# Splitting the products with C by a running difference, and loading batch norm rows over 128 partitions, in a four-layer hybrid kernel

## The chip, the cores and the metric

The kernel runs on one core of a Trainium2 chip. Its time is the time on the device, in microseconds. The kernel before the change took 6,203.77 us (median of three runs, 6,194.5 to 6,205.01). The engines are called PE (TensorE), DVE (VectorE), ACT (ScalarE), POOL (GpSimd) and SP (SyncE, which issues the DMAs here).

## What is computed

Four images of 96 channels and 64 x 64 pixels pass through four layers: a selective scan (layer 0), an inverted bottleneck with a depthwise convolution (layer 1), a spectral mixer with a quantised feed-forward (layer 2), and linear attention with another quantised feed-forward (layer 3). The change concerns layer 0's scan and the constants of layers 1 and 2. The scan, for each image, each of K = 4 directions, each of 192 channels d and 16 states n, over 4,096 positions:

```
dA  = exp(delta[d, t] * A[d, n])
h   = h * dA + (delta[d, t] * u[d, t]) * B[n, t]
y[d, t] = sum over n of h[d, n, t] * C[n, t]
```

The batch norms of layers 1 and 2 are affine maps that the kernel folds into the weights next to them: `s = g * rsqrt(v + eps)`, `t = b - m * s`, and then the weight matrix times `s` with `t` as one more row. As g, b, m and v are wanted along a matrix's columns, each is loaded as a row that is repeated over the partitions.

## The kernel before

**Units and steps.** The scan is cut into 64 steps: four images, four directions, four pieces of 1,024 positions. A step has 24 units, numbered u = 0 to 23. A unit is one tile of 128 partitions (32 channels by 4 states) by 1,024 positions, so there are 1,536 units. The loop `for slot in range(len(units) + 6)` (L1363) takes one unit a slot, in an order written out by hand (`manual_schedule`, L1493): each engine runs its instructions in the order in which this loop issues them.

**What a slot issues.** At slot s, in this order: on ACT `keep` (L1305), which copies the last column of unit s-1's state for the next piece, and the exponential of unit s+1 (`decays`, L1286), into one of two PSUM tiles (`da`); on POOL the input product g x B of unit s+2 (`inputs`, L1279), into one of eight tiles `w`; on POOL the product with C of unit s-2, if that unit is one of POOL's; on DVE the scan of unit s (`states`, L1293) and, if the unit is not POOL's, its product with C right behind (`product`, L1308); on PE the sums over states of a pair of units (`sums`, L1331), three slots after the pair's second unit. If a unit is POOL's, its states h are written over w in SBUF, and the product is made in place there; if it is DVE's, h is written over da in PSUM, and the product reads it there and writes w. Which units are POOL's is fixed before: `POOL_C` (L47) lists ten values of u, all even; the other fourteen are DVE's.

**Side work.** All other work (the input convolution and scan inputs of the next images, called the front stage; the convolution block; the spectral stages; layers 2 and 3) is written as generators that yield the engine and a planned time, as `yield dv(0.9)`. Stages follow each other in a plan (L1223). After each slot's own instructions, `advance` (L1454) takes side work whose engine has planned room left in this slot (`SHARE`, L58), up to a rate. The planned times (in us) steer the order alone. Behind the last scan only side work is left.

**The rows.** The first stage beside the scan is `weights` (`later_weights`, L324), which runs together with the group norm statistics of the three later images. It loads g1, b1, m1 and v1 as rows of 576 values and, in a second batch (L383), those of layer 2 as rows of 192 values, each repeated over C + 1 = 97 partitions, by `load_row` (L161), on SP's queue. The group norm statistics (`group_norm`, L509) load pieces of x (L502) and take `bn_stats` of them on DVE (L516).

Of the kernel before, what the change touches and what calls it, by code (L numbers as in the profile page):

```python
# [27 lines left out]
B, C, H, W = 4, 96, 64, 64  # L28
L = H * W
K, NS, R, DI = 4, 16, 6, 192  # L30
NE = R + 2 * NS
HID, NT1 = 576, 5
# [11 lines left out]
KORDER = [(0, 1, 3, 2)] * (B - 1) + [(1, 3, 0, 2)]  # L44

SCAN = {"d": 4, "g": 4, "B": 4, "C": 4, "w": 8}
POOL_C = (0, 2, 4, 6, 8, 12, 14, 16, 18, 20)  # L47
LAST = {"tab": 24, "more": 6}
TMP, IN = 9, 4

# [46 lines left out]
def hybrid_kernel(ctx: ExitStack, tc: tile.TileContext, a: dict):  # L97
# [10 lines left out]
    pool = lambda name, bufs=1, **kw: ctx.enter_context(tc.tile_pool(name=name, bufs=bufs, **kw))  # L108
# [52 lines left out]
    def load_row(out, name):  # L161
        load(out, a["rows"][:, ROW[name]].partition_broadcast(out.shape[0]))
        return out
# [32 lines left out]
    def big(name):  # L196
        if last_room and turns(thirds) == "last":
            return last_room[0].tile([128, 6144], F32, name=name, tag="big", bufs=1)
        return bp.tile([128, 6144], F32, name=name, tag="big", bufs=2)
# [86 lines left out]
    def scratch(t):  # L286

        at = 0

        def take(parts, *shape):  # L290
            nonlocal at
            n = int(np.prod(shape))
            at += n
            out = t[:parts, at - n : at]
            return out if len(shape) == 1 else out.rearrange("p (a b) -> p a b", b=shape[1])

        return take
# [26 lines left out]
    def later_weights():  # L324
# [3 lines left out]
        take = scratch(big("weights"))  # L328
        wo_a, wo_b = take(128, C), take(64, C)
        load(wo_a, a["wout_t"][0:128])  # L330
        load(wo_b, a["wout_t"][128:DI])
        s1, t1 = take(C + 1, HID), take(C + 1, HID)
        g1, b1, m1, v1 = (load_row(take(C + 1, HID), n) for n in ("g1", "b1", "m1", "v1"))
        g2r, v2r = load_row(take(128, C), "g2"), load_row(take(128, C), "v2")
        yield wait(4)
        yield pe(1.0, 1)
# [40 lines left out]
        take = scratch(big("weights"))  # L377
# [1 line left out]
        load(pre, a["pre"])  # L379
        w1t = take(C, DI)  # L380
        load(w1t, a["wa1_t"])
        sa, ta = take(C + 1, DI), take(C + 1, DI)
        ga, ba, ma, va = (load_row(take(C + 1, DI), n) for n in ("bn1_g", "bn1_b", "bn1_m", "bn1_v"))  # L383
        g, v = load_row(take(128, C), "bn2_g"), load_row(take(128, C), "bn2_v")
        load_row(rdid[0:64], "rd")
        load_row(rdid[64:128], "id")
# [3 lines left out]
        n = 2 * NG  # L390
# [35 lines left out]
        take = scratch(big("weights"))  # L426
# [27 lines left out]
    def flush():  # L454
        while to_store:
            out, t, then = to_store.pop(0)
            store(out, t)
            if then is not None:
                then()
# [772 lines left out]
    def scans(stages):  # L1232
# [13 lines left out]
        units = []  # L1246
        for number, step in enumerate(steps):
            u = 0
            for which, chans in enumerate(PASSES):
                for j in range(NJ):  # L1250
                    for i in chans:
                        units.append({"step": step, "number": number, "u": u, "j": j, "i": i, "pass": which,
                                      "pool": u in POOL_C})
                        u += 1

        def fetch(step, name, i):
            t = step[name][i] = wide(name)
            if name in "BC":
                lo = 4 * i + (NS if name == "C" else 0)
                of = d_bc[step["k"]][step["b"] % 3][step["c"], lo : lo + 4].unsqueeze(0)  # L1260
            else:
                of = (d_delta if name == "d" else d_du)[step["k"]][step["b"] % 3]
                of = of[step["c"], 32 * i : 32 * i + 32].unsqueeze(1)
            load(t, of.to_broadcast([32, 4, CH2]))

        def need(step):

            while not traced[step["b"]].issuperset((step["k"] % 2, 2 * step["c"] + e) for e in (0, 1)):
                force(stages)
            flush()  # L1270
# [6 lines left out]
        def inputs(x):  # L1277
            x["w"] = wide("w")
            nc.gpsimd.tensor_mul(x["w"], x["step"]["g"][x["i"]], x["step"]["B"][x["j"]])  # L1279

        def decays(x, last):
            if last is not None:
                keep(last)
            av = (x["step"]["k"] * NI + x["i"]) * NJ + x["j"]
            x["da"] = decay_banks()
            act(x["da"], x["step"]["d"][x["i"]], AF.Exp, scale=aneg[:, av : av + 1])  # L1286

        def states(x):
            step, u = x["step"], x["u"]
            order = slice(None, None, -1) if step["k"] >= 2 else slice(None)  # L1290
            x["h"] = x["w"] if x["pool"] else x["da"]
            start = 0.0 if step["n"] == 0 else steps[x["number"] - 1]["last"][:, u : u + 1]
            nc.vector.tensor_tensor_scan(  # L1293
                x["h"][:, order], x["da"][:, order], x["w"][:, order], start, ALU.mult, ALU.add
            )
            if not x["pool"]:
                product(x, nc.vector)
# [9 lines left out]
        def product(x, engine):  # L1307
            x["made"] = engine.tensor_mul(x["w"], x["h"], x["step"]["C"][x["j"]])  # L1308
# [31 lines left out]
        def sums_out():  # L1340
            while summed:
                group, y = summed.pop(0)
                step = group[0]["step"]
                yt = sp.tile([128, CH], F32, name="yt", bufs=1)
                nc.scalar.copy(yt, y)  # L1345
                which = group[0]["pass"]
                for e in (0, 1):
                    to = d_y[step["k"]][step["b"] % 2][2 * step["c"] + e]
                    later(to[64 * which : 64 * which + 64], yt[64 * e : 64 * e + 64],
                          (lambda b=step["b"]: through(b)) if which == len(PASSES) - 1 and e == 1 else None)  # L1350
# [12 lines left out]
        for slot in range(len(units) + 6):  # L1363
            clock[0] = slot
            x = units[slot] if slot < len(units) else None
            if x is not None:
                if x["u"] == 0:


                    last = len(units) - NST * PC  # L1370
                    if slot < last:
                        rate = max(RATE, sum(s.work for s in stages if s not in behind) / (last - slot))
                    else:
                        rate = sum(s.work for s in stages) / (len(units) - slot)
                for name, i in OWN.get(x["u"], ()):
                    fetch(x["step"], name, i)
                if x["number"] + 1 < len(steps) and x["u"] in LOADS:
                    if x["u"] == 14:
                        need(steps[x["number"] + 1])
                    for name, i in LOADS[x["u"]]:  # L1380
                        fetch(steps[x["number"] + 1], name, i)
            flush()
            if slot + 1 < len(units):
                decays(units[slot + 1], units[slot - 1] if slot > 0 else None)
            sums_out()
            if slot + 2 < len(units):
                inputs(units[slot + 2])
            if 2 <= slot < len(units) + 2 and units[slot - 2]["pool"]:
                product(units[slot - 2], nc.gpsimd)
            if x is not None:  # L1390
                states(x)
            for group in due.get(slot, ()):
                sums(group)
            for e, (us, most) in SHARE.items():
                room[e] = min(room[e] + us, most)
            tensor[0] = 0.0
            held_banks[0] -= freed[0]
            freed[0] = 0
            owed = min(owed + rate, 8.0)
            while owed > 0.0:  # L1400
                did = advance(stages)
                if did is None:
                    break
                owed -= did
        flush()


    clock, tensor = [-1], [0.0]
    room = {e: most for e, (_, most) in SHARE.items()}

    class Stage:
# [42 lines left out]
    def advance(stages):  # L1454

        while stages and not stages[0].fill():
            stages.pop(0)
        if stages:
            banks_left = BANKS["mm"] - held_banks[0]
            for stream in stages[0].active:  # L1460
                engine, us, banks, _ = stream["next"]
                if banks and banks > banks_left:

                    banks_left = 0
                elif fits(stream):
                    if engine != "wait":
                        room[engine] -= us
                    if engine == "pe":
                        tensor[0] += us
                    return stages[0].step(stream)  # L1470
        return None

# [175 lines left out]
```

## Time and profile before

| | |
|---|---|
| median of three runs | 6,203.77 us |
| the profiled execution | 6,203.38 us, its span 6,201.6 us |
| granted TensorE clock, mean | 0.85 |
| PE busy | 4,590.7 us (74%) |
| DVE busy | 5,318.7 us (86%) |
| ACT busy | 3,841.3 us (62%) |
| POOL busy | 5,069.5 us (82%) |
| products with C on POOL, on DVE | 640, 896 |

The page first gives busy time by engine, then the span in forty slices, the DMA queues, the chain of work that ended last, and the costliest groups of instructions. A group's row has the line, the engine, the operation, the tile written and those read, shapes and count; behind the first bar the busy time in us and the mean of one in ns; behind the second the idle time of the engine just before them, and what ended most of it. A row of the waits names the engine that waited and the line of its instruction, what ended the wait, and then the sum in us, the number of times and the longest. A row of the timeline has the start, the duration, the engine and the instruction, and in brackets the idle time before it; SPq is SP's queue, issuing DMAs.

### The profile page before, as it was taken

What the parts mean: (1) busy time and instruction counts of PE and PEld (TensorE: products, weight loads), DVE (VectorE), ACT (ScalarE), POOL (GpSimd) and SP (SyncE); (2) the same over time, 40 slices, a digit from 0 to 9 for tenths busy, and PEclk for the clock granted to TensorE, in tenths of its full rate; (3) what the DMA queues carried; (4) which work ended last, traced back from release to release, by engine and by line L of the source; (5) the groups of instructions that cost most, each with busy time, mean ns of one, the idle gap of its engine ahead of it and who ended that gap; (6) DMA issues with size and microseconds to landing.
All of it is one profiled execution on the core that took longest, in us unless ns stands there. A gap on an engine that the chain in (4) does not pass through costs nothing. (4 is left out here: it accounts for less than half of the span.)

```text
span 6201.6 us, 78736 instructions
## 1 busy us (share of the span) xinstructions
PE 4590.7 (74%) x27668; PEld 1692.7 (27%) x27668; DVE 5318.7 (86%) x3619; ACT 3841.3 (62%) x6056; POOL 5069.5 (82%) x2183
## 2 busy tenths in 40 slices
PE   6632867755888776686569878767898777678998
PEld 2100212210222542121012236321222542112284
DVE  4979899899999889989999998898999999898045
ACT  4742776764565577767546656777666667675335
POOL 4756878879999899988899998999999899898000
PEclk9765977867999888788779988888999888789999
DMA  5653566567654554456776445557754554674201
GB/s 180 218 168 120 193 201 202 195 213 226 218 167 155 188 166 150 157 189 200 228 228 198 155 149 187 174 174 221 228 162 154 176 183 157 194 223 131 71 13 40
DMA packets 424718, 1078.09 MB, mean 174 GB/s; under 512 B 79258, under 2 KB 81024, under 8 KB 423172
## 3 DMA queue, kind: packets, MB, share of 16 engines
q1 hardware_dynamic: 424324, 1073.06, 54.6%
q8 instruction: 220, 3.60, 0.2%
q14 instruction: 174, 1.43, 0.1%
HBM read 856.64 MB, written 220.66 MB: 174 GB/s over the span
## 5 line engine op out<-in xcount | busy, mean ns | idle before, releaser
L1279 POOL TENSOR_TENSOR scan_w<-scan_g,scan_B 128x1024 f32<-128x1024 f32 x1536 | 3607.5, 2377 | 370.9 <-PE ps_y L1331 281.6
L1286 ACT ACTIVATE ps_da<-scan_d,aneg 128x1024 f32<-128x1024 f32 x1536 | 1714.8, 1117 | 567.6 <-DVE scan_w L1293 294.4
L1293 DVE TENSOR_TENSOR_SCAN ps_da<-ps_da,state,scan_w 128x1024 f32<-128x1024 f32 x672 | 1576.3, 2346 | 199.9 <-ACT ps_da L1286 173.8
L1308 POOL TENSOR_TENSOR scan_w<-scan_w,scan_C 128x1024 f32<-128x1024 f32 x640 | 1519.5, 2374 | 274.3 <-ACT state L1305 163.9
L1331 PE MATMUL ps_y<-scan_w,cst 128*32 128x512 f32 x6144 | 993.2, 725 | 559.1 <-ACT yt L1345 195.7
L1308 DVE TENSOR_TENSOR scan_w<-ps_da,scan_C 128x1024 f32<-128x1024 f32 x896 | 1097.2, 1225 | 67.6 <-DMA scan_C<-bc 4.6
L1293 DVE TENSOR_TENSOR_SCAN scan_w<-ps_da,state,scan_w 128x1024 f32<-128x1024 f32 x480 | 1123.4, 2340 | 28.1 <-ACT ps_da L1286 25.5
L1293 DVE TENSOR_TENSOR_SCAN ps_da<-ps_da,scan_w 128x1024 f32<-128x1024 f32 x224 | 512.0, 2286 | 85.3 <-ACT ps_da L1286 66.8
L1331 PEld LDWEIGHTS ps_y<-scan_w,cst 128*32 128x32 f32 x6144 | 145.8, 117 | 1191.5 <-issue 642.1
L1305 ACT COPY state<-ps_da 128x1 f32<-128x1 f32 x672 | 106.9, 159 | 548.8 <-DVE scan_w L1308 547.3
L1293 DVE TENSOR_TENSOR_SCAN scan_w<-ps_da,scan_w 128x1024 f32<-128x1024 f32 x160 | 364.8, 2280 | 16.9 <-ACT ps_da L1286 9.6
L827 PE MATMUL ps_mm<-h,wd 128*32 128x512 f32 x3144 | 362.9, 593 | 9.0 <-ACT r L167 7.0
L565 PE MATMUL ps_mm<-xp,taps 128*128 128x512 f32 x576 | 292.3, 651 | 59.6 <-ACT xp L545 26.8
L804 PE MATMUL ps_mm<-wd,w 128*32 128x512 f32 x1944 | 241.8, 608 | 22.9 <-ACT h L808 10.7
L616 PE MATMUL ps_mm<-xd,dtw 128*128 128x512 f32 x256 | 167.6, 746 | 87.8 <-ACT z L638 50.3
L886 PE MATMUL ps_mm<-r,cst 128*128 128x512 f32 x220 | 151.0, 775 | 82.1 <-ACT r L883 25.8
L670 PE MATMUL ps_mm<-ya,cst 128*64 128x512 f32 x192 | 183.2, 1044 | 12.8 <-ACT acc L910 11.3
L631 DVE SCALAR_TENSOR_TENSOR ps_mm<-ps_mm,z 128x512 f32<-128x512 f32 x192 | 131.7, 686 | 68.4 <-ACT z L629 68.0
L625 ACT ACTIVATE z<-ps_mm 128x512 f32<-128x512 f32 x192 | 114.1, 594 | 121.9 <-PE ps_mm L620 60.2
L1000 PE MATMUL ps_mm<-wa,xp 128*64 128x96 f32 x1728 | 132.3, 311 | 66.0 <-DVE d L1009 37.5
L565 PEld LDWEIGHTS ps_mm<-xp,taps 128*128 128x128 f32 x576 | 115.3, 207 | 234.2 <-issue 158.4
L827 PEld LDWEIGHTS ps_mm<-h,wd 128*32 128x32 f32 x3144 | 104.3, 109 | 248.7 <-issue 210.9
(360 smaller groups left out, 6553.0 us busy)
## 6 DMA issues: line engine op xcount, KB each, us to landing
scan_g<-du SPq DMA_DIRECT2D x384, 512.0 KB, 4.8
scan_d<-delta SPq DMA_DIRECT2D x384, 512.0 KB, 6.0
scan_B<-bc SPq DMA_DIRECT2D x256, 512.0 KB, 5.0
scan_C<-bc SPq DMA_DIRECT2D x256, 512.0 KB, 5.6
y<-yt SPq DMA_DIRECT2D x384, 128.0 KB, 2.4
du<-g SPq DMA_DIRECT2D x128, 256.0 KB, 2.3
delta<-z SPq DMA_DIRECT2D x128, 256.0 KB, 2.4
tab<-in_etab SPq DMA_DIRECT2D x112, 256.0 KB, 4.6
```

The lines of the kernel that those rows point to most:

```text
L565: mm(p, lhsT=taps[:, t, 0:128], rhs=window(t, c + e), start=t == 0, stop=t == 8)
L616: mm(p, lhsT=dtw[:, o + 2 * third, 0:128], rhs=xd, start=True, stop=True)
L670: mm(split(p[:64]), lhsT=const("two")[:, :64], rhs=t[:, :L].rearrange("p (w h) -> p h w", h=H)[:, c * RPC : (c + 1) * RPC, :], start=True, ...
L804: mm(p[32 * n : 32 * n + 32], lhsT=w1[:, 32 * g : 32 * g + 32], rhs=xin[:, n : n + 15 : 2, 1 : W + 1], start=True, stop=True)
L827: mm(p[32 * n : 32 * n + 32], lhsT=held["wd"][:, groups[i], o, dx, :], rhs=here[i][:, :, dx : dx + W], start=dx == 0, stop=dx == 2)
L886: mm(v, lhsT=const("mean"), rhs=r, start=True, stop=True)
L1000: mm(p[s : s + 64, e * C : (e + 1) * C], lhsT=tok[:, g * 4 + e, :], rhs=wa1[:, hs], start=True, stop=True)
L1279: nc.gpsimd.tensor_mul(x["w"], x["step"]["g"][x["i"]], x["step"]["B"][x["j"]])
L1286: act(x["da"], x["step"]["d"][x["i"]], AF.Exp, scale=aneg[:, av : av + 1])
L1293: nc.vector.tensor_tensor_scan(x["h"][:, order], x["da"][:, order], x["w"][:, order], start, ALU.mult, ALU.add)
L1308: x["made"] = engine.tensor_mul(x["w"], x["h"], x["step"]["C"][x["j"]])
L1331: done = mm(y[32 * q : 32 * q + 32], lhsT=const("stack"), rhs=group[m]["w"][:, e * CH : e * CH + CH], start=first, stop=last)
```

## The change

The list `POOL_C` goes. At each unit `share` decides between the engines by a running difference, `ahead_by`: the planned work of DVE less that of POOL so far. A unit adds a scan on DVE (2.35) and an input product on POOL (2.37); its product with C adds 1.2 on DVE or 2.37 on POOL, and goes where the difference is left nearer to zero. The planned times of DVE's side work are added as `advance` takes them, and the difference is held within 6 us either way. Odd units can now be POOL's, and so can two units in a row. The order of all else is as before.

The rows of both batch norms, and the values s and t made of them, take 128 partitions in place of 97; only 97 of them are read.

```diff
-POOL_C = (0, 2, 4, 6, 8, 12, 14, 16, 18, 20)
+SCAN_US, PRODUCT_US = 2.35, (1.2, 2.37)
+AHEAD = 6.0
...
-        s1, t1 = take(C + 1, HID), take(C + 1, HID)
-        g1, b1, m1, v1 = (load_row(take(C + 1, HID), n) for n in ("g1", "b1", "m1", "v1"))
+        s1, t1 = take(128, HID), take(128, HID)
+        g1, b1, m1, v1 = (load_row(take(128, HID), n) for n in ("g1", "b1", "m1", "v1"))
...
-        sa, ta = take(C + 1, DI), take(C + 1, DI)
-        ga, ba, ma, va = (load_row(take(C + 1, DI), n) for n in ("bn1_g", "bn1_b", "bn1_m", "bn1_v"))
+        sa, ta = take(128, DI), take(128, DI)
+        ga, ba, ma, va = (load_row(take(128, DI), n) for n in ("bn1_g", "bn1_b", "bn1_m", "bn1_v"))
...
-                        units.append({"step": step, "number": number, "u": u, "j": j, "i": i, "pass": which,
-                                      "pool": u in POOL_C})
+                        units.append({"step": step, "number": number, "u": u, "j": j, "i": i, "pass": which})
...
+        def share(x):
+
+            on_vector, on_pool = PRODUCT_US
+            lead = ahead_by[0] + SCAN_US - on_pool
+            x["pool"] = abs(lead - on_pool) < abs(lead + on_vector)
+            lead += -on_pool if x["pool"] else on_vector
+            ahead_by[0] = max(-AHEAD, min(lead, AHEAD))
+
         def states(x):
             step, u = x["step"], x["u"]
+            share(x)
...
                 owed -= did
+                ahead_by[0] += beside[0]
+                beside[0] = 0.0
...
+    beside, ahead_by = [0.0], [0.0]
...
                     if engine == "pe":
                         tensor[0] += us
+                    if engine == "dve":
+                        beside[0] += us
```

## The prediction

> **What bounds the kernel now.** I read first the page's groups and its forty slices, then the stretches of time around what looked odd, then the waits, and last the issue queue. A stretch row holds start:end, its length, then the busy time of PE, PE's weight loads, DVE, ACT and POOL (count in brackets), granted clock, DMA share, GB/s. The groups:
>
> ```profile
> L1279 POOL TENSOR_TENSOR scan_w<-scan_g,scan_B 128x1024 f32<-128x1024 f32 x1536 | 3607.5, 2377 | 370.9 <-PE ps_y L1331 281.6
> L1308 POOL TENSOR_TENSOR scan_w<-scan_w,scan_C 128x1024 f32<-128x1024 f32 x640 | 1519.5, 2374 | 274.3 <-ACT state L1305 163.9
> L1308 DVE TENSOR_TENSOR scan_w<-ps_da,scan_C 128x1024 f32<-128x1024 f32 x896 | 1097.2, 1225 | 67.6 <-DMA scan_C<-bc 4.6
> ```
>
> A product with C is 1.225 us on DVE and 2.374 us on POOL; 640 of 1,536 lie on POOL. The scans themselves are 3,576 us of DVE (the four L1293 groups: 1576.3 + 1123.4 + 512.0 + 364.8). They run from 88.9 us to 5,724 us, so this phase is 5,635 of the 6,201.6 us. What follows is 477 us in which PE is busy for 441.8 us; the change doesn't touch it. Within the phase no engine is the bound throughout. Four steps (a step is 24 units) as stretches:
>
> ```profile
> 653.00:752.00 99.00, 81.81 (x293) 26.28 (x296) 86.71 (x61) 73.72 (x120) 83.04 (x36) 0.93 0.57 185
> 852.00:959.00 107.00, 69.41 (x172) 14.33 (x164) 104.19 (x80) 78.17 (x115) 79.37 (x34) 0.66 0.66 213
> 1506.00:1584.00 78.00, 46.84 (x142) 9.32 (x134) 72.18 (x41) 37.38 (x63) 78.00 (x35) 0.74 0.78 247
> 1663.00:1747.00 84.00, 83.33 (x478) 25.49 (x471) 75.94 (x47) 52.53 (x89) 84.00 (x37) 1.00 0.64 204
> ```
>
> In the second DVE is full (104.2 of 107) and POOL is not; in the third POOL is busy to the last nanosecond and DVE has 6 us free; in the fourth PE is full as well; in the first none is. The fixed pattern gives ten products to POOL in each. And there is a hole in which everything stands still:
>
> ```profile
> 391.96 30.19 SPq L162 DMA_DIRECT2D weights<-in_rows  x6
> 422.19 1.89 SPq L502 DMA_DIRECT2D x<-in_x  x3
> ...
> 432.74 1.88 DVE L516 BATCH_NORM_STATS2 st<-x 96x6 f32<-96x512 f32 x3 [36.77 <-DMA x<-in_x]
> ```
> ```profile
> 404.00:420.00 16.00, 0.00 (x0) 0.00 (x0) 0.00 (x0) 0.00 (x0) 0.00 (x0) 0.50 0.07 26
> ```
>
> The first rows are the timeline: six row loads held SP for 30.19 us, the x loads came out behind them, and DVE stood 36.77 us for x, with ACT (41.1 us) and POOL (40.9 us) behind it. The last row is the middle of that hole: a DMA share of 0.07 is one engine of sixteen (1/16 = 0.0625), at 26 GB/s. Four 218.2 KB loads at 26 GB/s are 34 us: the hole.
>
> **What the Trainium skill says.** (1) DMA: Bandwidth & Descriptors, section "Why a DMA increments its semaphore by 16 and not by 1": a transfer is spread over the largest number up to 16 that divides the outermost size, so 128 partitions use 16 engines and 127 one. 97 is a prime, which gives one; the trace agrees (0.07, 26 GB/s). (2) GPSIMD Engine Reference, section 1 "Specifications": POOL shares SBUF ports with DVE, contending with DVE instructions that have two SBUF inputs. DVE's product reads its h from PSUM, so neither placement should slow the other engine; queued POOL products follow each other at 2.32 us whatever DVE runs beside them, which agrees.
>
> **The change, part by part.** The sum is against the profiled execution's own 6,203.4 us, which equals the median shown (6,203.8).
>
> *Rows over 128 partitions.* Four loads grow from 218.2 to 288 KB and four (the second batch, L383) from 72.8 to 96 KB, now on sixteen engines. The trace has such a load: the taps, a row broadcast to 128 partitions, among other 128-partition loads at 20 to 30 us, where the slices show 391 to 409 GB/s. With the two 48 KB rows 1,248 KB at 390 GB/s is 3.2 us. SP then issues six at some 0.5 us each (the smallest issue of this line is 0.43), so x is issued at 395 instead of 422.2; x loads around there land 6.7 us after issue (median), so at 402. DVE is ready for x at 395.96, so it waits 6 us instead of 36.8: **31 us saved**. Between 25 (x takes 12 us, its wait behind other loads) and 35 (x lands in 2.0 us, the least in the trace). What is late next is x itself, then the scan loads queued behind it on SP. The second batch held SP for 13.67 us at 504, but DVE was busy 13.72 of the 14 us from 504 to 518: 0, at most the 2.9 us for which POOL waited for scan_B at 527. The Ln, Exp and products over 128 rather than 97 partitions keep their columns; durations here go by columns (128x1024 scan products, 96x512 at 0.68 against 128x512 at 0.69): 0, within 1 us.
>
> *The split.* The running difference needs no instruction on the chip. The changed program's order, which can be read without running it, has 676 products on POOL (+36): 401 units go from DVE to POOL and 365 back. Twenty-four steps get more than ten (up to 17 where the side work on DVE is dense; +70), 27 get fewer (7 to 9; -34). The order of the rest is the same. In totals it is worth nothing: POOL rises by 36 x 2.32 = 84 us to 5,139, DVE falls by some 41 to 5,089. What counts is each step's busier engine. I took for each of the 64 steps DVE's own busy time in the trace and 2.323 us for each POOL product (34 a step), and moved 1.15 us (a DVE product's time to the next instruction) and 2.323 us for each product that moves:
> - step at 852: ten to 17. DVE 105.0 to 97.0, POOL 79.0 to 95.2; busier engine -8.0.
> - step at 1506: ten to eight. POOL 79.0 to 74.3, DVE 69.9 to 72.2; -4.6.
> - all: 5,305 to 5,193, so **112 us**: 48 in the 21 steps where DVE is busier, 64 in the 43 where POOL is.
>
> That is not all to be had. In the steps of the front stage (ACT 70 to 80 us) the length follows DVE by half: from the step at 653 to that at 852 DVE's work rises by 18.7 us and the length by 9.2, so these waits, in which ACT, PE and DVE pass work round, take the rest: 24 of the 48. In POOL's 64 some steps are held by PE too (the fourth row above), and where two engines are equally full, each waits for the other now and then: I take half again, 32. The ends are 0 and 112. One wait is eased: in the program before, 198 exponentials (L1286) wait for the scan just ahead, all behind a POOL unit; in the trace DVE waits 195 times, 240.6 us in all, for an exponential. The changed program has 161 such. 37 x 1.23 = 46 us would be gained if DVE were always the last, which it isn't; I count it inside the half.
>
> *The wait added.* Before, POOL products stood only on the even unit of a pair, two slots ahead of the pair's sums (L1331). Now 339 of the 676 are on the odd unit, one slot ahead. PE stops at the sums until that product is there, and PE's side work, ACT's evictions behind it and then the next exponential wait. PE is 74% busy, which hides it; I count 0 and price it as a rival.
>
> Sum: 6,203.4 - 31 - 24 - 32 = **6,116 us**.
>
> **The rivals.**
> - *The whole 112*: the engines were only held by each other's bursts. POOL at 78.00 of 78 speaks for it; DVE's structural waits for ACT speak against. 6,203 - 31 - 112 = 6,060.
> - *Only the hole closes*: ACT's and PE's loops take the split's gain. For it: steps like the one at 653, where no engine is full and the step is 12 us longer than its busiest one. 6,203 - 31 = 6,172.
> - *The hole stays*: the x loads wait for something other than the single engine, say the ring. The share of 0.07 speaks against. 6,203 - 56 = 6,147.
> - *Slower, through PE*: the odd products hold up the sums.
>
> ```profile
> PE ps_y L1331 <- POOL scan_w L1308: 174.9, 59, 9.6
> ```
>
> Such a wait is 3.0 us (174.9/59). In the convolution stretches (1550 to 2015, 3255 to 3720, 4340 to 4805) PE is busy 1,192 of 1,395 us, 203 free, and 71 odd products fall in the steps there. To end over 6,216 this must undo 87 us and add 12 after using up the 203: 302/71 = 4.3 us for each. Only 59 of 640 waited before, so it needs nearly all to wait, and for longer.
>
> **How the numbers follow.** Forecast 0.56 (its own range 6,075 to 6,160), whole 112: 0.13, only the hole: 0.15, hole stays: 0.05, neither part shows: 0.04, slower: 0.07. Faster is 0.56 + 0.13 + 0.15 + 0.05 = 0.89, within 0.2% (12 us, about what a measurement of this kernel tells from no change) 0.04, slower 0.07. The range 6,056 to 6,180 takes in the forecast, the whole 112 with a hole of 35, and the hole alone; it leaves out a little over one in ten.
>
> **What would show it.** The row loads of the weights stage issued in 3 to 4 us instead of 30 and DVE's wait for x under 12 us; if it is still 30 the first step is wrong. The step at 852 some 4 us shorter with 17 POOL products and POOL busy over 90 us; the step at 1506 some 2 us shorter, with POOL no longer full. PE's wait for POOL's products at the sums: if it grows from 175 to over 400 us and the convolution steps are longer than 80 to 84 us, the rival through PE is at work. ACT and PE busy times stay; the last 477 us stay.

## The result, and the profile after

The changed kernel takes **6,126.6 us** (median of 4 runs, 6,121.9 to 6,131.0) against 6,204.4 us before, measured beside it: a ratio of **0.9876**, 95% interval 0.9858 to 0.9893. It is faster by 78 us; 87 us were forecast (6,203.4 to 6,116). The profiled execution has a span of 6,128.9 us, 72.7 us shorter than the 6,201.6 us before.

The page's groups, to be held against the three of before (busy time, mean ns of one, idle time ahead of them):

```profile
L1279 POOL TENSOR_TENSOR scan_w<-scan_g,scan_B 128x1024 f32<-128x1024 f32 x1536 | 3604.7, 2372 | 278.3 <-PE ps_y L1340 139.3
L1317 POOL TENSOR_TENSOR scan_w<-scan_w,scan_C 128x1024 f32<-128x1024 f32 x676 | 1603.8, 2372 | 217.1 <-ACT state L1314 160.4
L1317 DVE TENSOR_TENSOR scan_w<-ps_da,scan_C 128x1024 f32<-128x1024 f32 x860 | 1053.1, 1225 | 71.7 <-DMA scan_C<-bc 6.3
```

The counts are 676 and 860 as forecast, and the price of one product has moved on neither engine (2,372 and 1,225 ns). The four stretches of before, at the places where the same steps now lie:

```profile
621.00:717.00 96.00, 81.68 (x286) 26.07 (x284) 82.81 (x58) 73.35 (x119) 83.68 (x37) 0.93 0.57 187
816.00:917.00 101.00, 63.98 (x172) 13.55 (x172) 96.41 (x74) 79.09 (x118) 95.55 (x42) 0.75 0.70 223
1460.00:1537.00 77.00, 47.49 (x146) 10.26 (x147) 74.18 (x43) 37.78 (x63) 75.00 (x34) 0.76 0.80 258
1615.00:1699.00 84.00, 83.31 (x480) 25.41 (x479) 77.32 (x48) 53.72 (x91) 79.12 (x34) 1.00 0.65 195
```

The second row was 107 us with DVE at 104.2 and POOL at 79.4: now DVE and POOL are even, and the step is 6 us shorter. The third had POOL at 78.00 of 78: POOL now has 2 us free, DVE rose from 72.18 to 74.18, and the step is only 1 us shorter. In the fourth POOL dropped from 84.00 to 79.12 and nothing came of it: PE stands at 83.31 of 84. The timeline at the old hole:

```profile
385.35 2.95 SPq L163 DMA_DIRECT2D weights<-in_rows  x6
388.34 1.37 SPq L503 DMA_DIRECT2D x<-in_x  x3
...
394.70 2.22 DVE L517 BATCH_NORM_STATS2 st<-x 96x6 f32<-96x512 f32 x3 [10.21 <-DMA x<-in_x]
...
402.41 1.28 DVE L517 BATCH_NORM_STATS2 st<-x 96x6 f32<-96x512 f32 x2 [3.24 <-DMA x<-in_x]
```

The six row loads hold SP for 2.95 us instead of 30.19, and DVE waits 10.21 + 3.24 us for x instead of 36.77 + 2.0.

**Where the time went.** I laid the starts of the scans of both traces side by side, 24 to a step, and sorted the 64 steps as the prediction did: step 3 with the hole (it began at 394 us before), the 20 other steps in which DVE was the busier engine, and the 43 in which POOL was.

| | before, us | after, us | change | DVE busy, change | products on POOL |
|---|---|---|---|---|---|
| step 3 | 151.9 | 131.5 | -20.3 | +5.1 | 10 to 14 |
| 20 DVE-busier steps | 1,953.5 | 1,890.6 | -62.9 | -72.4 | 200 to 263 |
| 43 POOL-busier steps | 3,528.6 | 3,539.6 | +11.0 | +36.6 | 430 to 399 |
| whole scan phase | 5,634.0 | 5,561.8 | -72.3 | -30.7 | 640 to 676 |
| the end, after the scans | 478.6 | 477.8 | -0.8 | | |

The total came out, but not by the terms: the POOL-busier steps, priced at -32 us, gave nothing, and the DVE-busier ones, priced at -24 (step 3 among them), gave more than twice that. In 27 of the POOL-busier steps 34 products left POOL, 79 us of its work at 2.323 us each, and these steps together became 17 us longer. Some 8 us of the last two terms are no gain or loss of the split: with the rows alone (below), where no product moves, the DVE-busier steps read -7.3 and the POOL-busier ones +8.2.

**What DVE waited for.** A step's length is DVE's busy time plus its idle time, and the waits tell what ended the latter. Of the scans that write `da`, before and then after:

```profile
DVE ps_da L1293 <- ACT ps_da L1286: 240.6, 195, 5.0
...
DVE ps_da L1293 <- POOL scan_w L1279: 11.3, 14, 1.5
```
```profile
DVE ps_da L1302 <- ACT ps_da L1286: 213.4, 166, 4.9
...
DVE ps_da L1302 <- POOL scan_w L1279: 10.0, 8, 2.5
```

With the scans of POOL's own units, DVE waited 275.8 us for exponentials before and 253.7 after, and for POOL's input products 13.1 and 13.0 us. In the 43 POOL-busier steps of before it stood 295 us in all, 195 of them for exponentials and 11 for POOL. However busy POOL was, DVE was hardly ever kept waiting by it directly.

### The profile page after: what moved, and what is told of

It reads as the page before. It is cut to its first block, busy times and chain, and to the rows that moved or that the text cites. A ratio compares the mean times of both kernels' runs of the same rounds, so it can differ in the third digit from the quotient of the medians.

```text
span 6128.9 us, 78468 instructions
## 1 busy us (share of the span) xinstructions
PE 4611.9 (75%) x27668; PEld 1699.0 (28%) x27668; DVE 5286.9 (86%) x3583; ACT 3841.1 (63%) x6056; POOL 5157.5 (84%) x2219
## 5 line engine op out<-in xcount | busy, mean ns | idle before, releaser
L1279 POOL TENSOR_TENSOR scan_w<-scan_g,scan_B 128x1024 f32<-128x1024 f32 x1536 | 3604.7, 2372 | 278.3 <-PE ps_y L1340 139.3
L1317 POOL TENSOR_TENSOR scan_w<-scan_w,scan_C 128x1024 f32<-128x1024 f32 x676 | 1603.8, 2372 | 217.1 <-ACT state L1314 160.4
L1302 DVE TENSOR_TENSOR_SCAN ps_da<-ps_da,state,scan_w 128x1024 f32<-128x1024 f32 x633 | 1484.0, 2344 | 167.7 <-ACT ps_da L1286 143.8
L1340 PE MATMUL ps_y<-scan_w,cst 128*32 128x512 f32 x6144 | 1005.8, 734 | 597.7 <-POOL scan_w L1317 230.9
L1302 DVE TENSOR_TENSOR_SCAN scan_w<-ps_da,state,scan_w 128x1024 f32<-128x1024 f32 x519 | 1214.0, 2340 | 36.8 <-ACT ps_da L1286 35.3
L1317 DVE TENSOR_TENSOR scan_w<-ps_da,scan_C 128x1024 f32<-128x1024 f32 x860 | 1053.1, 1225 | 71.7 <-DMA scan_C<-bc 6.3
L1314 ACT COPY state<-scan_w 128x1 f32<-128x1 f32 x498 | 93.2, 187 | 180.7 <-DVE scan_w L1302 180.4
```

The costliest lines, as they stand in the source:

```text
L1302: nc.vector.tensor_tensor_scan(x["h"][:, order], x["da"][:, order], x["w"][:, order], start, ALU.mult, ALU.add)
L1314: nc.scalar.copy(step["last"][:, u : u + 1], x["h"][:, end : end + 1])
L1340: done = mm(y[32 * q : 32 * q + 32], lhsT=const("stack"), rhs=group[m]["w"][:, e * CH : e * CH + CH], start=first, stop=last)
```

## Experiments

All times stand against the kernel before, run beside them (6,203.8 to 6,206.5 us). Experiments start from one of the two kernels, as said with each.

**The rows alone** (from the kernel before; the fixed ten products stay), with two other heights of the tile:

```diff
-        s1, t1 = take(C + 1, HID), take(C + 1, HID)
+        s1, t1 = take(128, HID), take(128, HID)
```

and so for the other row tiles; 113 and 112 in the place of 128 for the second and third.

> The rows over 128 partitions, the split as before. Theory (97 rows ran on one DMA engine): DVE's wait for x at 396 us falls from 36.8 to 6 to 12 us and the whole shortens by that, to 6,173 to 6,182. Rival (what the hole gives back is taken later, since the front stage refills from the same loads): the hole closes but the time stays above 6,192.

> As before, but 113 partitions, also a prime. Theory (one engine): four loads of 113 x 2,304 bytes at 26 GB/s take 40 us in place of 34, so the hole grows from 36.8 to some 43 us and the time by 4 to 8 us, to about 6,210. Rival (the loads wait for something else, or 97 is special by its size): the hole stays within 2 us of 36.8, or shrinks, and the time is at or under 6,204.

> As before, but 112 partitions, seven times sixteen. Theory (the largest divisor up to 16 counts): sixteen engines, the hole is 6 to 12 us as with 128, time 6,173 to 6,182. Rival (a full 128 is needed): the hole stays over 25 us, time over 6,190.

| rows on | time, us | ratio | 95% interval |
|---|---|---|---|
| 128 partitions | 6,177.0 | 0.9946 | 0.9932 to 0.9959 |
| 113 | 6,213.3 | 1.0012 | 1.0006 to 1.0019 |
| 112 | 6,178.9 | 0.9953 | 0.9939 to 0.9966 |

The timelines of the three, in this order:

```profile
391.07 3.19 SPq L162 DMA_DIRECT2D weights<-in_rows  x6
394.31 1.37 SPq L502 DMA_DIRECT2D x<-in_x  x3
...
400.55 1.47 DVE L516 BATCH_NORM_STATS2 st<-x 96x6 f32<-96x512 f32 x2 [5.04 <-DMA x<-in_x]
```
```profile
390.76 35.49 SPq L162 DMA_DIRECT2D weights<-in_rows  x6
426.30 1.89 SPq L502 DMA_DIRECT2D x<-in_x  x3
436.84 1.88 DVE L516 BATCH_NORM_STATS2 st<-x 96x6 f32<-96x512 f32 x3 [41.41 <-DMA x<-in_x]
```
```profile
391.57 2.92 SPq L162 DMA_DIRECT2D weights<-in_rows  x6
394.54 1.37 SPq L502 DMA_DIRECT2D x<-in_x  x3
...
400.88 2.29 DVE L516 BATCH_NORM_STATS2 st<-x 96x6 f32<-96x512 f32 x3 [5.87 <-DMA x<-in_x]
```

One partition more or fewer decides: 113 is a prime like 97, and SP is held 35.49 us; 112 = 7 x 16 is as good as 128. The size of the load explains nothing, since 113 rows are less data than 128. This is what the Trainium skill's page "DMA: Bandwidth & Descriptors" (section "Why a DMA increments its semaphore by 16 and not by 1") says of the outermost size, and the runs agree: in the middle of the hole with 113 rows (404 to 420 us) the DMA share is 0.07 at 25 GB/s, as with 97. The hole's price is the time of step 3, 30.5 us less with 128, and 28 us of the whole. The waits for x there fell from 38.8 us to 7.1 in all, which is the whole of it: the second batch of rows, loaded in the same step, adds nothing. Of the other steps none before the fortieth moves by more than 2.0 us.

**The split alone** (from the changed kernel, the row tiles back on 97 partitions):

```diff
-        s1, t1 = take(128, HID), take(128, HID)
+        s1, t1 = take(C + 1, HID), take(C + 1, HID)
```

and so for the other row tiles.

> The running difference alone, rows over 97 partitions. Theory (two separate gains that add): the hole stays near 37 us and the rest of the gain is here, 78 less about 26, so some 6,150 (6,144 to 6,158). Rival (the two overlap: the split's gain in the weights stage needs the hole closed): over 6,165.

6,148.0 us, ratio 0.9903 (0.9890 to 0.9917): 57 us against the 6,205.0 run beside it, and with the 28 of the rows 85, against 78 measured for both. The parts add to within some 7 us. The hole was there (DVE waited 39.94 us for x). The POOL-busier steps: +4.7 us. And step 3 was 8.9 us *longer* than before, which no part of my working had.

**Products on even units only** (from the changed kernel): the running difference stays, but PE's sums never find a product just one slot ahead.

```diff
-            x["pool"] = abs(lead - on_pool) < abs(lead + on_vector)
+            x["pool"] = x["u"] % 2 == 0 and abs(lead - on_pool) < abs(lead + on_vector)
```

> The running difference, but only even units may be POOL's (640 again, none odd). Theory E: PE's wait for POOL's products is back at some 175 us or under, the step at 1,299 us at some 78 us; the steps that wanted 13 to 17 products stop at 12 and lose some 10 to 15 us in all; so 6,115 to 6,137. Rival (odd units cost nothing, so only the cap's loss is seen): 6,138 to 6,150.

6,159.7 us, ratio 0.9922 (0.9910 to 0.9935), 33 us slower than with the odd units and above both stated ranges. The waits of this kernel, and then of the changed one (in all, times, longest):

```profile
PE ps_y L1340 <- POOL scan_w L1317: 52.4, 25, 4.9
```
```profile
PE ps_y L1340 <- POOL scan_w L1317: 230.9, 79, 11.0
PE ps_y L1340 <- POOL scan_w L1279: 71.2, 17, 11.8
```

PE's wait for products with C is cut by 178 us when the odd ones go (the fixed ten, all even, had 174.9), and yet the kernel is slower: at most twelve products fit on even units, and the DVE-busier steps kept 26 of their 63 us. PE's wait is mostly hidden; the freedom to take any unit is not. The rival through PE does show in one place. In step 12, which begins at 1,299 us and grew from 77.5 to 84.7 us, the changed kernel's timeline reads:

```profile
1303.65 1.94 PE L1340 MATMUL ps_y<-scan_w,cst 128*32 128x512 f32 x8 [7.28 <-POOL scan_w L1317]
...
1307.54 0.60 ACT L626 ACTIVATE z<-ps_mm 128x512 f32<-128x512 f32 x1 [10.39 <-PE ps_mm L621]
...
1309.49 0.70 DVE L632 SCALAR_TENSOR_TENSOR ps_mm<-ps_mm,z 128x512 f32<-128x512 f32 x1 [7.25 <-ACT z L630]
```

PE waits for a POOL product, ACT for PE's side work, DVE for ACT: 7 us out of the step. The product is that of unit 23, the last of step 11, right behind another POOL product. It is this place that costs, and not odd products as such: the four kernels that give units 22 and 23 of step 11 to POOL have step 12 at 84.4 to 85.4 us, one of them (the next experiment) with the fixed even ten in step 12 itself. With even units alone it took 78.6 us, and in the last experiment, where step 11 ends otherwise and step 12 has six odd products in place of four, 77.5 us.

**The running difference in the front steps only** (steps 0 to 11 and 28 to 31; the list `POOL_C` is put back for the others):

```diff
+            if not (x["number"] < 12 or 28 <= x["number"] < 32):
+                x["pool"] = x["u"] in POOL_C
```

> The running difference in the 16 steps of the weights and front stages alone (the first 12, and four from 2,674 us on); the fixed even pattern in the other 48. Theory from the two traces (the other 48 steps gain 12 us in all): 6,135 to 6,145. Rival (the prediction's 32 us in those steps): 6,155 or more. A third case (they gain nothing or lose): 6,130 or less.

6,144.7 us, ratio 0.9899 (0.9885 to 0.9912), at the upper end of the theory's range. The running difference in the other 48 steps is worth 18 us of the whole, 20 us by their lengths. Six of them were DVE-busier before (20, 21, 39, 41, 53, 55), and in the changed kernel these six alone are 24 us shorter than here. The remaining 42 are 4 us longer (3,451 us against 3,447): the split gains nothing there.

**Later sums, and POOL's state copies.** Three kernels on the two waits that looked next in line: the sums one slot later, everywhere or in the front steps alone, and the state copy of POOL's units on POOL, ahead of the product, instead of on ACT.

```diff
-            when = at + 3
+            when = at + 4
```
```diff
+            number = group[0]["number"]
-            when = at + 3
+            when = at + (4 if number < 12 or 28 <= number < 32 else 3)
```
```diff
-                nc.scalar.copy(step["last"][:, u : u + 1], x["h"][:, end : end + 1])
+                copy = nc.gpsimd.tensor_copy if x["pool"] else nc.scalar.copy
+                copy(step["last"][:, u : u + 1], x["h"][:, end : end + 1])
...
-            if last is not None:
+            if last is not None and not last["pool"]:
...
+                keep(units[slot - 2])
                 product(units[slot - 2], nc.gpsimd)
```

> The changed kernel with the sums of each pair issued one slot later, so that an odd POOL product again stands two slots ahead of them. Theory E (the new wait of PE for odd products costs time, as in the step at 1,299 us, which got 7 us longer): PE's wait for POOL's products at the sums falls below 150 us from 231, that step falls back to some 78 us, and the time to 6,095 to 6,118. Rival F (the eight w tiles are held longer, so POOL waits for them instead): POOL's wait for the sums grows from 139 to over 300 us and the time is 6,127 or more.

> The changed kernel with the copy of a POOL unit's last column moved from ACT to POOL itself, just ahead of the product that overwrites it: some 498 short copies more on POOL, and no wait of POOL for ACT (160 us in the changed kernel, 140 times). Theory (POOL's waits for ACT are on the path in the front steps): the wait disappears and the time falls to 6,085 to 6,115. Rival (POOL's own time counts most): at an estimated 0.1 to 0.2 us each, after the 0.1 us of POOL's 128x1 memsets, the copies add 50 to 100 us to POOL, and the time stays within 10 us of 6,127 or rises.

> The changed kernel with the sums one slot later in steps 0 to 11 and 28 to 31 only. Late sums everywhere shortened these steps by 15 us (7 of them may be work that only moved to the step ahead) and lengthened the other 48 by 40. Theory (a longer-held scan_w tile costs only where POOL is short of time, so the two effects can be had apart): the front steps lose 8 to 15 us, the others stay within 5 us, 6,112 to 6,120 us in all. Rival (the gain in the front steps was chance in the placing of side work, and anything moves it by so much): within 5 us of the changed kernel, or slower.

> Late sums in the front steps only, and the state copy of POOL's units made by POOL ahead of the product instead of by ACT. Alone the second edit gave 6 us. Theory: the two add up, 15 to 20 us below the changed kernel, 6,106 to 6,114 us. Rival (POOL has no time left in the front steps, so its copies there eat the gain of the late sums): no faster than the better of the two alone, 6,115 to 6,121 us.

| edit | time, us | ratio | 95% interval |
|---|---|---|---|
| none (the changed kernel) | 6,126.6 | 0.9876 | 0.9858 to 0.9893 |
| late sums everywhere | 6,155.4 | 0.9917 | 0.9904 to 0.9931 |
| copies on POOL | 6,120.4 | 0.9861 | 0.9847 to 0.9874 |
| late sums in front | 6,135.0 | 0.9881 | 0.9866 to 0.9897 |
| late in front, and copies | 6,138.7 | 0.9895 | 0.9879 to 0.9912 |

Late sums everywhere lose 29 us, all of it in the POOL-busier steps (+40.7 us against +11.0). They cut PE's wait, and POOL waits longer, since each scan_w tile comes free a slot later. The waits with late sums, and after that of the changed kernel:

```profile
POOL scan_w L1279 <- PE ps_y L1340: 265.2, 133, 8.7
...
PE ps_y L1340 <- POOL scan_w L1317: 193.8, 67, 8.2
```
```profile
POOL scan_w L1279 <- PE ps_y L1340: 139.3, 81, 7.7
```

That POOL's wait is the path by which the 29 us are lost isn't shown: DVE's scans waited 8.3 us for POOL's input products, less than the 13.0 of the changed kernel, and 16 us more for exponentials. Confined to the front the late sums were to give 8 to 15 us there. The front steps of that trace are 2.1 us shorter, and the whole isn't faster. This is the rival's case, that the 15 us which late sums everywhere had shown there came by chance, from where side work falls. The copies on POOL did end POOL's wait for ACT, 160 us in the changed kernel, but cost POOL 94 us (498 of 189 ns), and the time fell by 6 us where 12 to 42 were the theory. Nor do the two edits add up: together they are no faster than either alone, and slower than both stated ranges. The 6 us of the copies are unproved too, for when work ahead merely shifts in time, steps here move by as much: with late sums in front, steps 20, 24, 41 and 59, which that edit doesn't touch, moved by -7, -7, +6 and -14 us.

**The ten fixed products in step 3 alone** (the running difference everywhere else). This is about the 9 to 10 us that the split had cost in step 3.

```diff
+            if x["number"] == 3:
+                x["pool"] = x["u"] in POOL_C
```

> The changed kernel with the old fixed ten products on POOL in step 3 alone. Step 3 lost about 10 us to the running difference (121.4 us with the rows alone, 131.5 us with both): four products fewer on DVE, 4.9 us, but the small group norm and weight operations of DVE there took 53.0 us instead of 44.2, 19 batch norm statistics among them unchanged, and the wait for x was 6.3 us longer because the step began earlier. Theory A (small DVE operations with both inputs in SBUF stand behind a running POOL product, some 2.2 us each, and a busier POOL catches more of them): with ten products the small operations fall back to 44 to 47 us, the products cost 4.9 us again, the wait for x stays; step 3 at 126 to 129 us, the whole 2 to 5 us faster. Rival B (the odd products hold up PE and the group norm chain there): the small operations stay near 53 us and the step falls to 121 to 124 us, or, if neither, it stays at 131 to 136 us.

6,112.8 us, ratio **0.9849** (0.9834 to 0.9864), the fastest of all by its median; its interval overlaps that of the changed kernel, and of the 15 us between the two profiles only 4 lie in step 3. Step 3 took 127.3 us against 131.5, as theory A had it, and the small operations of DVE took 44.2 us. Over all kernels of this study they go by the number of products on POOL in step 3:

| products on POOL in step 3 | DVE's other operations there, us |
|---|---|
| 10 (before, the three with the rows alone, this one) | 41.1 to 44.2 |
| 12 (even units only) | 46.7 |
| 14 (the changed kernel and six variants of it) | 51.7 to 53.0 |

These are the durations, added up, of every DVE instruction of the step that is neither a scan nor a product with C: 49 instructions in each kernel. The groups of the changed kernel, kept apart by shape:

```profile
L372 DVE TENSOR_TENSOR w<-w,weights 128x576 f32<-128x576 f32 x1 | 2.8, 2849 | 0.0
L369 DVE COPY w<-weights 1x576 f32<-1x576 f32 x1 | 2.5, 2489 | 0.0
L178 DVE TENSOR_TENSOR t<-cols,t 96x1 f32<-96x1 f32 x1 | 2.3, 2264 | 0.0
```

and those of the kernel with ten fixed in step 3, where these lines have other numbers:

```profile
L373 DVE TENSOR_TENSOR w<-w,weights 128x576 f32<-128x576 f32 x1 | 0.8, 758 | 0.0
L370 DVE COPY w<-weights 1x576 f32<-1x576 f32 x1 | 0.5, 456 | 0.0
L179 DVE TENSOR_TENSOR t<-cols,t 96x1 f32<-96x1 f32 x1 | 0.2, 155 | 0.0
```

The same operation on one element in each of 96 partitions takes 155 ns or 2,264 ns. The changed kernel's timeline shows beside what:

```profile
451.60 2.34 POOL L1317 TENSOR_TENSOR scan_w<-scan_w,scan_C 128x1024 f32<-128x1024 f32 x1 [2.78 <-DVE scan_w L1302]
451.70 2.85 DVE L372 TENSOR_TENSOR w<-w,weights 128x576 f32<-128x576 f32 x1
...
453.90 2.86 POOL L1279 TENSOR_TENSOR scan_w<-scan_g,scan_B 128x1024 f32<-128x1024 f32 x1
```

DVE's operation was issued 0.1 us behind POOL's product and ended 0.6 us after it (454.55 against 453.94): it stood until POOL was nearly or quite done, and then took about the 0.76 us that it takes elsewhere. POOL's next product, begun while DVE was still at work, took 2.86 us in place of 2.3. In this trace 31 such DVE operations that read SBUF alone (the batch norm instructions apart) began while a POOL product of either kind ran; 30 of them ended only when it was done, and the other had begun together with it. This is in the Trainium skill: "SBUF — State Buffer", section "SBUF: two separate sides", has VectorE and GpSimd share a port pair that whichever starts first holds for its whole instruction, where the VectorE operation has two inputs in SBUF, and GpSimd's reads SBUF too, or is in a two-port mode. The runs agree: the operations that stood take two inputs from SBUF, or copy, cast or scale within it; the scans (2.33 us) and DVE's own products (1.22 us), which take one input from PSUM, kept their times, and so did the batch norm statistics (0.66 to 0.69 us), which have a single input in SBUF. That the copies and casts were in a two-port mode no run here shows.

## Why the prediction was right, and where it wasn't

- **Hole, 31 us: right.** SP free in 3 us, x issued at 394.3 us (395 said), there at 400.5 (402 said), DVE's first wait 5.04 us (6 said) with the rows alone; 28 us of the whole. With the split as well the waits are 13.5 us in all, since DVE reaches step 3 some 13 us earlier and x isn't there: part of what the split wins in steps 0 to 2 is handed back here. That the second batch of rows is worth 0 was right.
- **DVE-busier steps, 24 us: right in kind, mis-sized.** The 20 of them apart from step 3 gave 63 us (56 against the rows alone); the whole difference of the busier engines, step 3 among them, is only 48. Two things were wrong. The busier engine charged POOL's rise against the gain, and halving it took the rest: I had read the slope of length on DVE's work between two steps with different side work, where ACT and PE differ too. In the step at 852 the two engines went where I put them (DVE 96.4, 97.0 said; POOL 95.6, 95.2 said), and the step lost 6.8 us where 4 was said. The length followed DVE's own work: in these 20 steps it fell by 28, 59 and 72 us with even units only, with the front steps only and in the changed kernel, and the steps by 26, 45 and 63. DVE's waits gave nothing there (161 us idle before, 170 after; for exponentials 81 and 76), though I had put a gain of theirs inside the half.
- **POOL-busier steps, 32 us: this step failed.** I took POOL's 78.00 busy of 78 for the bound, and the busier engine for the pace of every step. In 27 such steps 79 us of work were taken from POOL, and the steps grew by 17 us; all 43 gave +11 us. Against before, the 43 gave +11.0 in the changed kernel and +4.7, +7.4, -3.5, +8.1 and -9.2 in five variants that split them nearly alike (the split alone, copies on POOL, late sums in front, these two together, step 3 fixed), and +8.2 to +9.4 in the three where no product moves: nothing, give or take 10. The trace of before could have told. In these 43 steps POOL was busy 3,374 of 3,529 us, full in about a dozen of them, and DVE waited for it 11 us; the 79.0 us that I gave POOL in each is longer than eight of the steps. (The 69.9 us given to DVE in the step at 1506 should be the 72.18 of the row.) Every product taken back from POOL is DVE's work again: DVE's busy time rose by 37 us and its idle time fell by 26, which are the 11. Why the idle time isn't less, some 270 us of which 177 are waits for exponentials, and whether POOL has a part in it through PE and ACT, is open. In some steps PE is full too (83.3 of 84, which the prediction saw).
- **The wait added, 0: right for the whole, not everywhere.** PE's wait for POOL's products with C grew from 174.9 to 230.9 us, not to 400 (that for its input products from 21.8 to 71.2). Taking it away again with even units alone didn't pay. The last product of step 11 costs 7 us in step 12.
- **Not in the working at all: the port.** The prediction had named the contention for DVE instructions with two SBUF inputs and cleared DVE's *product* of it; it never asked it of the small operations already there. That queued POOL products follow each other at 2.32 us *whatever* DVE runs beside them was read too widely: in the trace of before four of them took 2.85 to 3.45 us, each beside such an operation. A busier POOL added 14 us to DVE's operations over the run (814.8 to 828.7 us), 9 to 10 of it in step 3.

So the sum came near by luck: mis-sized terms lie on opposite sides. By the lengths of the steps, against the 87 us said: 39 more from the DVE-busier steps, 43 less from the POOL-busier ones, 6 less from the hole (25 us by the waits for x in step 3), and 5 lost net in step 3 itself: 87 + 39 - 43 - 6 - 5 = 72, the 72.3 us by which the scan phase shortened.

## What to carry to other kernels

An engine at 100% in a stretch is not yet its bound: see who waits for it before pricing what leaves it. Here the engine to follow was DVE, which waited 13 us for POOL's input products in 5,634, and the DVE-busier steps followed DVE's own work. When work is moved to GpSimd, look up every small VectorE instruction beside it that has two inputs in SBUF, or copies and casts within it, not only the moved one. A row broadcast wants a number of partitions divisible by 16, as 112 and 128 were here and 97 and 113 were not, even where the extra rows are never read.

## What the runs showed that was not expected

- A DVE operation on 96x1 elements took 155 or 2,264 ns, and one on 128x576 758 or 2,849 ns, by whether a POOL product of 2.37 us was running when it began.
- A row broadcast to 113 partitions held the issuing queue 35.49 us, to 112 partitions 2.92 us.
- Single steps of this kernel moved by 6 to 14 us where only the work ahead of them had shifted in time. One profile of such a kernel can't tell an edit worth 10 us from chance, and the times of four runs barely can.
